# Set-up loads and steps in another order: a convolution, attention and mixture-of-experts kernel on one core

## The chip, the core and the metric

The kernel runs on one core of a Trainium2 chip. A core has a matrix engine (TensorE, PE in the profile), a vector engine (VectorE, DVE), an activation engine (ScalarE, ACT), a general engine (GpSimd, POOL) and a queue engine (SyncE, SP) that mainly issues DMAs. Each engine runs its own instructions in order, and waits on semaphores for what other engines and DMAs produce. ScalarE and GpSimd can issue DMAs too, from their own instruction streams.

The metric is the device time of one execution in microseconds (us). Before the change it is 3165.85 us, the median of three runs (3164.92 to 3170.51).

## What is computed

The input x is 8 images of 56 x 56 positions with 256 channels. Layer 0 sends it through 32 parallel paths, each a 1x1 convolution to 4 channels, a 3x3 convolution in these 4, and a 1x1 convolution back to 256, each followed by a batch norm and a ReLU, and adds up the paths and x. Layer 1 normalises, applies a linear attention over the positions of one image, normalises again and sends every position to the best 2 of 8 experts. Cut to what matters:

```
h = relu(bn1(x @ w1 + b1))                  # per path, 256 -> 4
h = relu(bn2(conv3x3(h, w2) + b2))          # per path, 4 -> 4
h = relu(bn3(h @ w3 + b3))                  # per path, 4 -> 256
x = relu(sum of h over the 32 paths + x)
t = x as tokens; n = layer_norm(t)
t = t + n + q @ (k^T v / N)                 # 8 heads, q = n, k and v normalised per head
t = t + moe(layer_norm(t))                  # router, best 2 of 8 experts, gelu
```

## The kernel before

**Tiling.** The 8 images are cut into 56 chunks of 8 rows, 448 positions each. Work runs in slots, one per chunk (the loop `for s in range(S + A + 1)` near the end of the function). Slot s computes the third convolution of chunk s (`pair`, L643 to L653, and `sum_paths`, L664), and beside it the first convolution of chunk s+2 (`conv1_steps`), the taps and the second convolution of chunk s+1 (`spread_taps`, `conv2_steps`), and, from the ninth slot on, attention and experts of earlier chunks. So before slot 0 can start, the set-up has to do the first convolution of chunks 0 and 1 and the second convolution of chunk 0, beside preparing all the weights.

**Order.** On TensorE, ScalarE and VectorE the instructions stand in the order in which the code issues them (`manual_schedule`). On SyncE and GpSimd a scheduler places them, by when it reckons that their inputs are there. Each of these two then also runs strictly in the order that came out.

**The set-up, in the code's order.**
- First weights W1 and the batch-norm rows are loaded, and `load(0)` (L87) loads the first chunk; `load` is called again in `conv1_steps` for the next chunk as soon as a chunk has been transposed. There is one input buffer (`xin`, one tile), so a load also waits for TensorE's transposes (L276) of the chunk before.
- GpSimd makes `ident` and the masks (`group_mask`, L138 to L143), the powers of the batch norms (L157), later the zero borders of h1 (L251 to L254), `path_mask` and `picks`.
- V3, G3, B3, M3, Be3 and W3 are loaded (L200, L215), VectorE works out scale and shift of the third batch norm, and the results are re-laid by eight small DMAs to `g3` and `bias3` (L206).
- The second weights come as twelve small DMAs to `W2s` (L233), 32 rows of 3 times 4 numbers each, 1.5 KB; VectorE spreads them into `W2t` (L241).
- `all_of(conv1_steps(0), conv1_steps(1))` (L353) runs the first convolutions (transposes L276, copies L279, products L287, activation L290 into `h1`), and `spread_taps(0)` copies shifted rows of h1 to the taps `R` with three DMAs (L310), two by SyncE and one by ScalarE.
- The third weights follow: `tp_mask` (L379), `spread`, `tp_g3` (L383), `W3s` (L384), products `tp_w3` (L390, L391), `W3hl` (L392).
- Then the biases of the third batch norm: `pmod`, `pdiv`, `b4` (L403 to L414) on VectorE, `tp_b3` (L419) on TensorE, `b3t` and `nb3` (L423, L424).
- Only then comes `all_of(conv2_steps(0))` (L425): twelve products (L323), the activation to `h2` (L332), its halves `hi` and `lo` (L340, L341), which four DMAs (L345) re-lay into `hl` for the third convolution: the two of lo by ScalarE, the two of hi by SyncE.
- `tp_sb` (L429) and `sumb`, and the output biases of the experts: `b2s` is loaded (L438), split into `b2hl` and `b2l`, and b2l stored into b2hl by a DMA (L441). With that the memory of the set-up is given back, and later tiles, `r` of L647 among them, are placed in it.
- Loads that attention needs: `kw_c`, `kb_c` (L461), `vw_b`, `vb_b` (L466), and the router weights `rwc` (L477), which are centred by four products with `mean_of` (L480) and two subtractions (L482).

Of the kernel before, what the change touches and what calls it, by code (L numbers as in the profile page):

```python
# [8 lines left out]
F32 = mybir.dt.float32  # L9
# [4 lines left out]
ALU = mybir.AluOpType  # L14
# [7 lines left out]
SYNC = mybir.DependencyInfo(mybir.DependencyClass.Sync, mybir.DependencyReason.DATA)  # L22
# [3 lines left out]
def kernel(  # L26
# [24 lines left out]
    nc = tc.nc  # L51
    B, N, C = x.shape
# [3 lines left out]
    E = w1.shape[0]  # L56
    HC = 32
    NH = C // HC
    P = 128
    NF = C // P  # L60
# [18 lines left out]
    ps_mm = ctx.enter_context(tc.tile_pool(name="ps_mm", bufs=7, space=PSUM))  # L79


    xs_in = {}

    def load(s):
        b, c = divmod(s, NCH)
        X = xin.tile([T, KT, C], F32, tag="xi", name=f"xi_{s}")
        nc.sync.dma_start(  # L87
            out=X, in_=x[b, c * CH : (c + 1) * CH, :].rearrange("(k q) c -> q k c", q=T)
        )
        xs_in[s] = X  # L90

    xtp = ctx.enter_context(tc.tile_pool(name="xtp", bufs=4))
# [15 lines left out]
    for g in range(NG):  # L108
        nc.scalar.dma_start(
            out=bn2s[32 * g : 32 * g + 32],  # L110
            in_=bn2[32 * g : 32 * g + 32].rearrange("(a e) k -> e a k", a=4),
# [118 lines left out]
    W2s = setup.tile([3 * 32, NG, 3, D], F32, name="W2s")  # L230
    for dx in range(3):
        for g in range(NG):
            nc.sync.dma_start(  # L233
                out=W2s[dx : 3 * 32 : 3, g],
                in_=W2[32 * g : 32 * g + 32].rearrange(
                    "q (dy dx o) -> dx q dy o", dy=3, dx=3
                )[dx],
            )
# [20 lines left out]
    def all_of(*parts_of_slot):  # L259
        for steps in parts_of_slot:  # L260
            for _, fn in steps:
                fn()
# [52 lines left out]
    def conv2_steps(s):  # L315
        ps = []

        def taps_of(dy):
            if dy == 0:
                ps.append(ps_mm.tile([P, 512], F32, tag="mm", name=f"c2_{s}"))  # L320
            R = tapped[s]
            for g in range(NG):
                nc.tensor.matmul(  # L323
                    ps[0][32 * g : 32 * g + 32, :CH],
                    W2t[:, g, dy, :],
                    R[:, g, :].rearrange("q (r w) -> q r w", w=W58)[:, dy : dy + ROWS, :HW],
                    start=(dy == 0), stop=(dy == 2),
                )
            if dy == 2:
                del tapped[s]  # L330
                h2 = split.tile([P, CH], F32, tag="h2", name=f"h2_{s}")
                nc.scalar.activation(h2, ps[0][:, :CH], AF.Relu, bias=sh2, scale=sc2)  # L332
                h2s[s] = h2

        def halves():

            h2 = h2s[s]
            hi = split.tile([P, CH], F32R, tag="hi", name=f"hi_{s}")
            lo = split.tile([P, CH], F32R, tag="lo", name=f"lo_{s}")
            nc.vector.tensor_copy(hi, h2)  # L340
            nc.vector.tensor_tensor(lo, h2, hi.bitcast(F32), ALU.subtract)  # L341
            hl = hlp.tile([P, NQ, CH], F32R, tag="hl", name=f"hl_{s}")
            for v, part in enumerate((hi, lo, hi, lo)):
                queue = nc.scalar if s == 0 and v % 2 else nc.sync
                queue.dma_start(out=hl[v : P : 4, :, :].bitcast(F32), in_=part.bitcast(F32))  # L345
            h2s[s] = hl

        return [
            (0.8, lambda: taps_of(0)), (0.8, lambda: taps_of(1)), (0.8, lambda: taps_of(2)),
            (0.8, halves),  # L350
        ]

# [25 lines left out]
    tp = ps_mm.tile([P, 512], F32, tag="mm", name="tp_mask")  # L378
# [3 lines left out]
    tp = ps_mm.tile([P, 512], F32, tag="mm", name="tp_g3")  # L382
# [5 lines left out]
    for ab in range(NQ):  # L388
        tp = ps_mm.tile([P, 512], F32, tag="mm", name=f"tp_w3_{ab}")
# [8 lines left out]
            ALU.mult,  # L398
        )


    pmod = setup.tile([NP, NPL], F32, name="pmod")
    nc.vector.tensor_reduce(  # L403
# [12 lines left out]
        )  # L416
    tp = ps_mm.tile([P, 512], F32, tag="mm", name="tp_b3")
    for cg in range(NCG):
        nc.tensor.matmul(  # L419
            tp[:, cg * 8 : cg * 8 + 8],  # L420
            b4[:, cg].rearrange("q p c -> q (p c)"), pdiv, start=True, stop=True,
        )
    nc.vector.tensor_copy(b3t, tp[:, : NCG * 8].rearrange("q (g n) -> q g n", n=8))  # L423
    nc.vector.tensor_scalar_mul(nb3, b3t, -1.0)  # L424
    all_of(conv2_steps(0))  # L425

    for f in range(NF):
        tp = ps_mm.tile([P, 512], F32, tag="mm", name=f"tp_sb_{f}")
# [26 lines left out]
    tables = ctx.enter_context(tc.tile_pool(name="tables", bufs=1))  # L455


    def column(src, name):

        t = const.tile([P, NF], F32, name=name)  # L460
        nc.sync.dma_start(out=t, in_=src.rearrange("o (f c) -> c (o f)", c=P))  # L461
        return t

    def bcast(src, name):
        t = const.tile([P, C], F32, name=name)
        nc.sync.dma_start(out=t, in_=src.to_broadcast([P, C]))  # L466
        return t

    kw_c, kb_c = column(kw, "kw_c"), column(kb, "kb_c")
# [3 lines left out]
    mean_of = const.tile([P, P], F32, name="mean_of")  # L473
    nc.gpsimd.memset(mean_of, 1.0 / C)

    rwc = const.tile([P, NF, E], F32, name="rwc")
    nc.sync.dma_start(out=rwc, in_=rwT.rearrange("(f c) e -> c f e", c=P))  # L477
    tp = ps_mm.tile([P, 512], F32, tag="mm", name="tp_rw")
    for f in range(NF):
        nc.tensor.matmul(tp[:, :E], mean_of, rwc[:, f, :], start=(f == 0), stop=(f == NF - 1))  # L480
    for f in range(NF):
        nc.vector.tensor_sub(rwc[:, f, :], rwc[:, f, :], tp[:, :E])  # L482

# [74 lines left out]
    for e in range(M):  # L560
# [6 lines left out]
        out=below, in_=below, compare_op=ALU.is_ge, fill=0.0, base=-1,  # L567
# [8 lines left out]
        out=earlier, in_=earlier, compare_op=ALU.is_ge, fill=0.0, base=-1,  # L576
# [919 lines left out]
    for s in range(S + A + 1):  # L1496
        a = s - A
        work_of = []
        era = " alone" if s < A else ""
        if s <= S:  # L1500
            work_of.append((0.0, 1.0 if is_chunk(s) else 0.1, conv3_steps(s)))
        if is_chunk(s + 2):
            work_of.extend(at("conv1" + era, conv1_steps(s + 2)))
        if is_chunk(s + 1):
            work_of.extend(at("taps" + era, [(0.0, lambda: spread_taps(s + 1))]))
            work_of.extend(at("conv2" + era, conv2_steps(s + 1)))
        if is_chunk(s - 1):
            if s < S:
                work_of.extend(at("end" + era, end_steps(s - 1)))
            else:  # L1510
                work_of.append((0.12, 0.99, end_steps(s - 1)))
        if is_chunk(a + 1):
            work_of.extend(at("fetch", [(0.0, lambda: fetch(a + 1))]))
        if is_chunk(a):
            opens = a % NCH == 0
            if opens:
                work_of.extend(at("image", image_steps(a // NCH)))
            if a + A > S:
                work_of.extend(at("attention first last" if opens else "attention last", attn_steps(a)))
            else:  # L1520
                work_of.extend(at("attention first" if opens else "attention", attn_steps(a)))
        work_of.extend(left)
        left = []
        if waiting and (len(waiting) == 2 or waiting[-1] % NCH == NCH - 1):
            last_image = waiting[-1] >= S - NCH
            compute, scatters = route_steps(waiting)
            rt = places["route" if s < S else "route last"]
            work_of.append((rt[0], rt[1], compute))
            if last_image:
                work_of.append((places["scatter last"][0], 0.995, sum(scatters, [])))  # L1530
            else:
                work_of.append((places["scatter"][0], 0.995, scatters[0]))
                left = [(0.0, places["scatter"][1], steps) for steps in scatters[1:]]
            if waiting[-1] in closing:
                work_of.append((places["plan"][0], places["plan"][1], plan_steps(closing.index(waiting[-1]))))
            waiting = []
        while r + 1 < len(closing) and known_in[r + 1] <= s:
            r += 1
        if r >= 0 and r + 1 < len(closing):
            goal = upto + (known_after[r] - 2 - upto) // (known_in[r + 1] - s)  # L1540
            if r + 2 < len(closing):
                goal = min(known_after[r] - 2, goal if s < known_in[1] else tiles_by(s))
            work_of.append((places["tiles"][s <= known_in[r]], places["tiles"][2], moe_steps(upto, goal)))
            upto = goal
        if 1 <= s <= E:
            work_of.append((0.5, 0.5, [(0.0, lambda: copy_weights(s - 1))]))
            work_of.append((0.8, 0.8, [(0.0, lambda: empty_rows(s - 1))]))
        if s == S + 1:
            apart.append(s)
        issue(*work_of)  # L1550
        if is_chunk(a):
            waiting.append(a)
# [60 lines left out]
```

## Time and profile before

| What | Value |
|---|---|
| median of three runs | 3165.85 us |
| the profiled execution | 3194.13 us |
| its span, first to last instruction | 3192.3 us |
| mean granted clock of TensorE, share of full | 0.962 |
| scatters on GpSimd, L1120 | 448, 957 ns each |
| adding scatters on GpSimd, L1413 | 420, 1573 ns each |

The span is what the profile's times are counted in; the profiled execution is somewhat longer than an execution without a profile. Stretches of the set-up, us busy of each engine, with the clock that TensorE was granted:

| Stretch, us | PE | DVE | ACT | POOL | PE clock |
|---|---|---|---|---|---|
| 0 to 13 | 4.96 | 5.83 | 3.07 | 9.83 | 1.00 |
| 13 to 26 | 5.22 | 3.46 | 2.04 | 2.58 | 0.61 |
| 26 to 40 | 10.14 | 7.61 | 0.00 | 0.00 | 0.70 |
| 40 to 53 | 7.07 | 2.68 | 1.87 | 0.00 | 0.50 |
| 53 to 83 | 28.66 | 20.03 | 18.25 | 0.00 | 0.90 |

In the first four stretches the load passes from engine to engine, and TensorE is busy 27.4 of 53 us. In the fifth, slot 0, TensorE is busy nearly throughout.

In the profile's lines a name such as `c`, `h` or `tx` is a program's tile name with its numbers left out, so c stands for the first, second and third convolution alike, and the line number tells them apart. SPq and ACTq mark the issuing of DMAs by SyncE and ScalarE. A 32-bit matrix product is recorded in two passes, so the twelve products L323 appear as `x24`.

### The profile page before, as it was taken

What the parts mean: (1) busy time and instruction counts of PE and PEld (TensorE: products, weight loads), DVE (VectorE), ACT (ScalarE), POOL (GpSimd) and SP (SyncE); (2) the same over time, 40 slices, a digit from 0 to 9 for tenths busy, and PEclk for the clock granted to TensorE, in tenths of its full rate; (3) what the DMA queues carried; (4) which work ended last, traced back from release to release, by engine and by line L of the source; (5) the groups of instructions that cost most, each with busy time, mean ns of one, the idle gap of its engine ahead of it and who ended that gap; (6) DMA issues with size and microseconds to landing.
All of it is one profiled execution on the core that took longest, in us unless ns stands there. A gap on an engine that the chain in (4) does not pass through costs nothing.

```text
span 3192.3 us, 53679 instructions
## 1 busy us (share of the span) xinstructions
PE 2924.8 (92%) x16677; PEld 1663.9 (52%) x16677; DVE 2173.6 (68%) x5743; ACT 1919.8 (60%) x3827; POOL 1844.5 (58%) x1363
## 2 busy tenths in 40 slices
PE   6999888888999999999999999999999997887798
PEld 3334334333455555455555555555555555776677
DVE  4787887787877687776877777777778784433200
ACT  2666665556666666566666766566656654454455
POOL 1233254455566675756756666666663556677677
PEclk7999998899999999999999999999999998998899
DMA  2543344344556666667665766667756666898897
GB/s 68 156 127 123 120 133 127 112 146 152 158 163 163 190 175 177 168 177 192 184 184 155 203 184 169 179 164 197 191 161 181 176 160 152 210 250 205 202 223 179
DMA packets 322669, 537.53 MB, mean 168 GB/s; under 512 B 41152, under 2 KB 232784, under 8 KB 322384
## 3 DMA queue, kind: packets, MB, share of 16 engines
q1 hardware_dynamic: 239808, 429.91, 44.4%
q0 software_dynamic: 81984, 103.45, 17.8%
q8 instruction: 133, 2.18, 0.3%
q14 instruction: 152, 1.25, 0.1%
q10 hardware_dynamic: 592, 0.76, 0.1%
HBM read 248.01 MB, written 192.55 MB: 138 GB/s over the span
## 4 chain that ended last, share of the span: by engine, by line
PE 68%; DVE 10%; issue 4%; ACT 3%; POOL 3%; DMA 2%; another core or an unknown queue 0%; ACTq 0%; SPq 0%; POOLq 0%; DVEq 0%
PE c L643 12%; PE ph L1375 11%; PE su L664 11%; PE py L1395 9%; PE at L939 7%; PE kv L813 3%; DVE r L651 3%; PE te L1335 3%; PE c L323 2%; PE py L1391 2%; POOL hsd L777 2%; PE c L287 2%; ACT r L648 2%; PE tu L712 1%; PE tx L276 1%
## 5 line engine op out<-in xcount | busy, mean ns | idle before, releaser
L651 DVE SCALAR_TENSOR_TENSOR r<-c,nb,r 128x448 f32<-128x448 f32 x1792 | 1131.2, 677 | 446.4 <-ACT r L648 414.4
L648 ACT ACTIVATE r<-c,b3t 128x448 f32<-128x448 f32 x1792 | 1038.5, 634 | 333.0 <-PE c L643 314.9
L1413 POOL DMA_INDIRECT out_dram<-y,index x420 | 660.5, 1573 | 342.7 <-ACT y L1399 221.5
L643 PE MATMUL c<-hl,W3hl 64*128 64x448 f32 x3584 | 690.4, 427 | 52.7 <-ACT r L648 19.3
L1120 POOL DMA_INDIRECT regions<-pay,rrowi x448 | 428.9, 957 | 311.9 <-PE c L643 198.5
L664 PE MATMUL su<-r,gather 128*32 128x448 f32 x3584 | 558.0, 566 | 42.8 <-DVE r L651 34.6
L643 PEld LDWEIGHTS c<-hl,W3hl 64*128 64x128 f32 x3584 | 328.2, 188 | 482.6 <-issue 242.0
L1375 PE MATMUL ph<-eT,w 128*128 128x256 f32 x1680 | 453.2, 401 | 38.1 <-issue 15.1
L1399 ACT ACTIVATE y<-py,rows 128x256 f32<-128x256 f32 x420 | 196.7, 474 | 438.9 <-PE py L1395 327.8
L1395 PE MATMUL py<-w,hT 128*128 128x256 f32 x1680 | 432.0, 381 | 7.0 <-issue 6.3
L1375 PEld LDWEIGHTS ph<-eT,w 128*128 128x128 f32 x1680 | 306.0, 196 | 169.0 <-issue 77.0
L1379 ACT ACTIVATE hT<-ph,w 128x256 f32<-128x256 f32 x420 | 197.9, 476 | 252.2 <-PE ph L1375 127.6
L777 POOL TENSOR_TENSOR hsd<-hsd,half 112x36 f32<-112x36 f32 x49 | 303.3, 6190 | 70.5 <-DVE hsd L775 69.6
L1395 PEld LDWEIGHTS py<-w,hT 128*128 128x128 f32 x1680 | 290.3, 191 | 36.6 <-issue 7.5
L939 PE MATMUL at<-tab,tT 128*112 128x272 f32 x896 | 266.2, 421 | 15.1 <-ACT r L648 6.1
L738 POOL TENSOR_TENSOR norm<-t,hmean 112x512 f32<-112x512 f32 x112 | 121.4, 1164 | 245.5 <-PE c L643 125.0
L664 PEld LDWEIGHTS su<-r,gather 128*32 128x32 f32 x3584 | 101.6, 109 | 250.2 <-DVE r L651 107.9
L939 PEld LDWEIGHTS at<-tab,tT 128*112 128x112 f32 x896 | 150.8, 182 | 94.1 <-issue 33.1
L943 DVE SCALAR_TENSOR_TENSOR X<-at,rs,X 112x256 f32<-112x256 f32 x224 | 107.0, 478 | 122.4 <-PE at L939 60.8
L1391 PE MATMUL py<-b2hl,own 128*128 128x256 f32 x420 | 179.1, 426 | 6.7 <-ACT y L1399 2.8
L1065 POOL TENSOR_TENSOR rq<-ebase,rq 112x8 f32<-112x8 f32 (+1 forms) x32 | 51.2, 1600 | 227.0 <-DVE rq L1064 227.0
L1339 ACT COPY eT<-te 128x512 f32<-128x512 f32 x210 | 123.5, 588 | 60.5 <-PE te L1335 40.6
(261 smaller groups left out, 3160.4 us busy)
## 6 DMA issues: line engine op xcount, KB each, us to landing
w<-Wd SPq DMA_DIRECT2D x210, 513.0 KB
rows<-regions SPq DMA_DIRECT2D x210, 259.0 KB
xi<-in_x_dram SPq DMA_DIRECT2D x56, 448.0 KB
hl<-hi SPq DMA_DIRECT2D x112, 224.0 KB
tTs<-u SPq DMA_DIRECT2D x56, 448.0 KB
ts<-t SPq DMA_DIRECT2D x56, 448.0 KB
tT<-tTs SPq DMA_DIRECT2D x56, 448.0 KB
X<-ts SPq DMA_DIRECT2D x56, 448.0 KB
```

Source lines behind the costliest of these rows:

```text
L643: product = nc.tensor.matmul(tiles[g][:, :CH], W3hl[rows, ab, cg, :], hl[rows, ab, :], start=True, stop=True)
L648: nc.scalar.activation(r, tiles[0][:, :CH], AF.Relu, bias=b3t[:, cg, 2 * ab : 2 * ab + 1])
L651: nc.vector.scalar_tensor_tensor(r, tiles[1][:, :CH], nb3[:, cg, 2 * ab + 1 : 2 * ab + 2], r, op0=ALU.max, op1=ALU.add,)
L664: nc.tensor.matmul(ps[32 * c4 : 32 * c4 + 32, :CH], gather, unit.pop((s, 4 * u + c4)), start=(ab == 0), stop=(ab == NQ - 1),)
L777: nc.gpsimd.tensor_tensor(sd, sd, half[:T, :].rearrange("q (k h) -> q k h", k=KT), ALU.pow)
L939: nc.tensor.matmul(ps, tT[:, f, k * T : (k + 1) * T], tables_of[b][:, f, :], start=(f == 0), stop=(f == NF - 1),)
L1120: ins = nc.gpsimd.indirect_dma_start(out=regions[n], out_offset=bass.IndirectOffsetOnAxis(ap=v["row_i"][:, (m - group[0]) * KT + k, n : n ...
L1375: nc.tensor.matmul(ps, w[:, f * C + hf * P : f * C + (hf + 1) * P], eT[:, f, :], start=(f == 0), stop=(f == NF - 1),)
L1379: nc.scalar.activation(hT[:, hf, :], ps, AF.Gelu, bias=w[:, 2 * NF * C + hf : 2 * NF * C + hf + 1])
L1391: nc.tensor.matmul(ps, own.to_broadcast([P, P]), b2hl, start=True, stop=False)
L1395: nc.tensor.matmul(ps, hT[:, f, h * P : (h + 1) * P], w[:, (NF + f) * C : (NF + f + 1) * C], start=False, stop=(f == NF - 1),)
L1413: ins = nc.gpsimd.indirect_dma_start(out=out_rows, out_offset=at, in_=y[:, h, :], in_offset=None, compute_op=ALU.add, **partial,).ins
```

## The change

The twelve loads of W2s are issued by GpSimd instead of SyncE. The second convolution of chunk 0 is put ahead of the biases of the third batch norm. The load of chunk 3 waits for the `lo` half of chunk 0 (`halved`), and the loads of kw_c, kb_c, vw_b, vb_b and rwc wait for the last product of tp_b3 (`last_made`). The router's centring becomes a function that is called at the start of slot 1. Nothing of what is computed changes.

```diff
@@ load(s)
-        nc.sync.dma_start(
+        ins = nc.sync.dma_start(
             out=X, in_=x[b, c * CH : (c + 1) * CH, :].rearrange("(k q) c -> q k c", q=T)
-        )
+        ).ins
+        if s == 3:
+            tc.add_manual_dep(ins, halved[0].name, SYNC, reason="not needed by the first chunk")
@@ second weights
     for dx in range(3):
         for g in range(NG):
-            nc.sync.dma_start(
+            nc.gpsimd.dma_start(
                 out=W2s[dx : 3 * 32 : 3, g],
@@ conv2_steps, halves
-            nc.vector.tensor_tensor(lo, h2, hi.bitcast(F32), ALU.subtract)
+            ins = nc.vector.tensor_tensor(lo, h2, hi.bitcast(F32), ALU.subtract).ins
+            if s == 0:
+                halved.append(ins)
@@ after W3hl, ahead of pmod
+    all_of(conv2_steps(0))
...
-        nc.tensor.matmul(
+        product = nc.tensor.matmul(
             tp[:, cg * 8 : cg * 8 + 8],
             b4[:, cg].rearrange("q p c -> q (p c)"), pdiv, start=True, stop=True,
         )
+    last_made = product.ins
...
     nc.vector.tensor_scalar_mul(nb3, b3t, -1.0)
-    all_of(conv2_steps(0))
@@ loads of attention and router
+    def not_yet(ins):
+
+        tc.add_manual_dep(ins, last_made.name, SYNC, reason="not needed by the first chunk")
...
-        nc.sync.dma_start(out=t, in_=src.rearrange("o (f c) -> c (o f)", c=P))
+        not_yet(
+            nc.sync.dma_start(out=t, in_=src.rearrange("o (f c) -> c (o f)", c=P)).ins
+        )
...
-        nc.sync.dma_start(out=t, in_=src.to_broadcast([P, C]))
+        not_yet(nc.sync.dma_start(out=t, in_=src.to_broadcast([P, C])).ins)
...
-    nc.sync.dma_start(out=rwc, in_=rwT.rearrange("(f c) e -> c f e", c=P))
-    tp = ps_mm.tile([P, 512], F32, tag="mm", name="tp_rw")
-    for f in range(NF):
-        nc.tensor.matmul(tp[:, :E], mean_of, rwc[:, f, :], start=(f == 0), stop=(f == NF - 1))
-    for f in range(NF):
-        nc.vector.tensor_sub(rwc[:, f, :], rwc[:, f, :], tp[:, :E])
+    not_yet(nc.sync.dma_start(out=rwc, in_=rwT.rearrange("(f c) e -> c f e", c=P)).ins)
+
+    def center_router():
+        tp = ps_mm.tile([P, 512], F32, tag="mm", name="tp_rw")
+        for f in range(NF):
+            nc.tensor.matmul(tp[:, :E], mean_of, rwc[:, f, :], start=(f == 0), stop=(f == NF - 1))
+        for f in range(NF):
+            nc.vector.tensor_sub(rwc[:, f, :], rwc[:, f, :], tp[:, :E])
@@ the loop over slots
+        if s == 1:
+            center_router()
```

More of the change, by code (lines that the diff above doesn't have):

```diff
@@ L82 @@
     xs_in = {}
+    halved = []
     def load(s):
```

## The prediction, made before the changed kernel had run

> **What bounds the kernel now.** I read the engine table of the page first. TensorE is busy 92% of the span, VectorE 68%, ScalarE 60%, so what counts in the long middle is the order of TensorE's work, and the change leaves that alone. The clock row comes next: one slice of forty, the first, stands out.
>
> ```profile
> PE 2924.8 (92%) x16677; PEld 1663.9 (52%) x16677; DVE 2173.6 (68%) x5743; ACT 1919.8 (60%) x3827; POOL 1844.5 (58%) x1363
> PEclk7999998899999999999999999999999998998899
> ```
>
> A slice is 80 us, and the set-up lies in the first. The chain of waits cannot be followed into it (its first piece is at 294 us), so the timeline of the first 60 us carries the case. Columns: start, length, engine, line, operation; in brackets the idle time before it.
>
> ```profile
> 7.66 7.71 SPq L233 DMA_DIRECT2D W2s<-in_W_dram  x12
> 15.48 0.52 SPq L87 DMA_DIRECT2D xi<-in_x_dram  x1
> 19.12 1.76 PE L276 MATMUL tx<-ident,xi 112*128 112x112 f32 x8 [7.91 <-DMA xi<-in_x_dram]
> 23.90 0.42 PE L379 MATMUL tp_mask<-ident,path_mask 128*32 128x128 f32 x1
> 26.71 0.42 DVE L384 TENSOR_TENSOR W3s<-W3s,tp_g 128x256 f32<-128x256 f32 x1 [8.68 <-PE tp_g L383]
> 35.90 3.55 PE L419 MATMUL tp_b<-pdiv,b 32*128 32x8 f32 x16 [2.92 <-DVE b L414]
> 39.38 4.71 PE L323 MATMUL c<-R,W2t 96*32 96x448 f32 x24
> 44.16 0.73 ACT L332 ACTIVATE h<-c,sh,sc 128x448 f32<-128x448 f32 x1 [18.24 <-PE c L323]
> 47.01 0.34 SPq L87 DMA_DIRECT2D xi<-in_x_dram  x1
> 47.45 1.34 SPq L345 DMA_DIRECT2D hl<-hi  x2
> 52.91 1.12 PE L643 MATMUL c<-hl,W3hl 64*128 64x448 f32 x4 [5.93 <-DMA hl<-hi]
> ```
>
> The reader sees three delays, one after another. Twelve W2s issues hold SP for 7.71 us, so the second chunk's input is issued at 15.48 and TensorE stands idle until 19.12. The first second convolution (L323) runs behind the bias products (L419) though its taps R were issued at 24.93. And the copies of its result (hl) leave SP behind a 448 KB input load, so the first third-convolution product waits 5.93 us. From 52.91 on, work is steady: TensorE busy 28.7 of the next 30 us.
>
> [...] a scatter (L1120) takes 0.95 us with 0.30 us to the next, an adding scatter (L1413) 1.57 and 0.30. No direct one is in this trace. [...] L323's 24 records take 4.71 us at 39.38 (granted clock 0.50) and 2.46 us at 71.62 (1.00).
>
> **The change, part by part.**
>
> *W2s leaves SP.* 7.71 us of issuing go from SP; input 1 is then released by TensorE's eight transposes of input 0 (done at 7.99) and issued at about 8.1. In the trace it takes 3.6 us from issue to transpose (15.48 to 19.12), so 11.7; L276 to the end of h1's second part takes 24.87 - 19.12 = 5.75, so 17.5 in place of 24.87.
>
> *W2s on GpSimd.* In the built order the twelve stand between bn1's power (L157) and the four borders of h1 (L251 to L254); behind these come path_mask and picks. The first taps (R) wait for the borders, tp_mask for path_mask, so all of them now wait for the twelve issues. Price: [...] a plain DMA of 96 short pieces is nearest to the 112-row scatter, 0.95 + 0.30 = 1.25, less its index; I take 1.1. Twelve make 13.2 us. From the end of bn1's power at 5.24: 13.2 + the four small ones left between them (0.30 + 0.25 + 0.57 + 0.25) = 19.9. Then borders 0.5, path_mask 0.23, picks 0.94, first select 0.53, own 0.2, second select 0.53: path_mask is ready at 22.8, where TensorE used to take it at 23.90. So GpSimd takes SP's place as the limit, about one microsecond earlier.
>
> *From the mask to W3.* tp_mask to W3s is 26.71 - 23.90 = 2.81 now; ScalarE's copy between them starts 1.35 us after tp_mask's end, because a taps issue (0.68) and h1 stand before it. Both are now over by 21.2, which gives 1.25 back: 22.9 + 2.81 - 1.25 = 24.45. VectorE arrives in time: W2t ends near 22.4, picks (0.90) 23.3, own4 24.0, all by the rows of before. W3s is 2.3 us early; so is the end of tp_w3 (6.27 us later): 30.7. Taps issued at 20.4 to 21.7 take at most 6 us (24.93 to about 31 with other loads): 27, in time.
>
> *Second convolution ahead of biases.* From tp_w3's end at 30.7, TensorE's clock is already up (the products at 31.95 to 32.98 take 0.6 where the first take 1.06), so I take 2.46 for L323, 4.71 if not: 33.2. h2 34.05, hi 34.5, lo 35.1. VectorE then makes pmod, pdiv and b4: 1.33 (34.43 to 35.76), 36.5. tp_b3 0.1 + 3.5: 40.1. The transposes of bias3 and chunk 2 take 46.97 - 44.02 - 0.87 (tp_rw, moved out) = 2.1: 42.3. The first L643 starts at 42.3 in place of 52.91, 10.6 early; 8.4 with the slow clock.
>
> *Loads held back.* hl is issued from 34.5 with no input load ahead. Before, 1344 KB (hl and an input) took 46.01 to 52.9; 896 KB at that rate plus the start take about 6 us: 40.6, hidden by tp_b3 with 1.7 us over. The column and broadcast loads wait for tp_b3 (40.1), and b2hl's store follows them on SP: four issues take 2.45 (27.25 to 29.70), it is issued at 42.6, and lands near 45. The first ScalarE r (L648) writes where b2l lay and so waits for it; it would want to start at 43.2. What is queued behind it is r 1 and then h1 of chunk 2, which must wait anyway for L287's 3.35 us (to 46.8). Two r (1.16) from 45 end at 46.2, so it is hidden by 0.6; up to 1.1 us is lost if L287 runs at full rate, which itself saves 1.6. Input 3 is issued near 44 and used 30 us later: nothing.
>
> *Router centring in slot 1.* Four products and two subtractions, 1.02 us at half clock, 0.5 at full: at most 0.5 back.
>
> Sum: 10.6, less 0.5 for slot 1, less 0.3 as a small share of the 2.2 us that a slow clock in L323 would cost: 9.8 us. On the profile's own time: span 3192.3 to 3182.5 (with what lies around it, 3194.13 to 3184.3). The runs' median lies 0.9% below the profiled execution; the set-up is a fixed stretch at the start, so I subtract the same from it: 3165.85 - 9.8 = 3156.0. All later waits are relative (product to activation, slot to slot), so a shift of the start goes to the end whole.
>
> **Rivals.**
>
> Dearer GpSimd issues. Each 0.1 us adds 1.2 to path_mask. At 1.5 to 1.87 the mask comes 4.8 to 9.2 later than reckoned and the gain is 5 to 0.6: about 3162.5. For it: the adding scatter's 1.87. Against: it has 128 rows and an addition.
>
> Cheaper issues. At 0.7 the mask is there at 18.0 and SP's own row (g3, bias, input 2, then R at 19.3) and R's landing near 26 become the limit as well (tp_w3 would end at 25.9): a gain near 14.6, 3151.
>
> [...]
>
> The start is shifted but the time is not: 3165.85. For it: the chain of waits shows nothing before 294 us. Against: TensorE's 28.7 busy of 30 us right after the set-up.
>
> **How the numbers follow.** Forecast (gain 6.5 to 13) 0.60; cheaper 0.12; dearer 0.17; no shift 0.05[...]. A measurement of this kernel can tell about 0.2%, 6.3 us, from no change. Faster by more: 0.60 + 0.12 = 0.72; within it 0.17 + 0.05 = 0.22; slower 0.06. The range takes the cheap case's 14.6 and a little run-to-run spread on one side, and all but the end of the dear one (1.4) on the other: 3150.5 to 3164.5.
>
> **What would show it.** Right: input 1's transposes near 12 us; POOL rows for W2s with a pitch near 1.1; tp_mask near 23; L323 near 31 in 2.5 us, tp_b near 36.5; first L643 near 42; first r near 45. Wrong: a pitch over 1.5, an idle ScalarE before h1 of chunk 2 because b2hl is late, or slot 0 starting early while slot 8 does not.

## The result, and the profile after

| | Before | After |
|---|---|---|
| median of all runs, 7 each | 3167.61 us (3164.92 to 3172.83) | 3150.42 us (3146.32 to 3159.09) |
| profiled execution | 3194.13 us | 3157.97 us |
| its span | 3192.3 us | 3156.2 us |
| mean granted clock | 0.962 | 0.966 |

After over before is 0.9949, with a 95% interval of 0.9935 to 0.9964: about 16.2 us of 3167.6 less, between 11 and 21. The two medians are 17.2 us apart. The forecast was a gain of 9.8. The median, 3150.42, lies 0.1 us under the low end of the stated range (3150.5). So not the case held most likely came (a gain of 6.5 to 13), but the rival with cheaper issues, held at 0.12, which had put the time at 3151.

The same timeline as before, now of the changed kernel (columns: start, length, engine, line, operation; in brackets the idle time before it). Its lines are 3 to 16 higher: L323 became L326, L419 L425, L643 L657, L648 L662.

```profile
7.97 5.43 POOL L236 DMA_DIRECT2D W2s<-in_W_dram  x10
7.95 0.33 SPq L88 DMA_DIRECT2D xi<-in_x_dram  x1
11.86 0.99 PE L279 MATMUL tx<-ident,xi 112*128 112x112 f32 x8 [0.71 <-DMA xi<-in_x_dram]
13.09 1.77 PE L290 MATMUL c<-xT,W1s 128*128 128x448 f32 x4 [0.24 <-ACT xT L282]
16.15 0.30 PE L384 MATMUL tp_mask<-ident,path_mask 128*32 128x128 f32 x1 [1.29 <-POOL path_mask L146]
17.53 0.42 DVE L389 TENSOR_TENSOR W3s<-W3s,tp_g 128x256 f32<-128x256 f32 x1 [0.37 <-PE tp_g L388]
17.98 1.46 DVE L391 CAST W3h<-W3s 128x256 fp32r<-128x256 f32 x1
25.95 2.46 PE L326 MATMUL c<-R,W2t 96*32 96x448 f32 x24
29.66 1.20 SPq L350 DMA_DIRECT2D hl<-hi  x2
31.59 3.27 PE L425 MATMUL tp_b<-pdiv,b 32*128 32x8 f32 x16 [3.18 <-DVE b L420]
36.73 1.11 PE L657 MATMUL c<-hl,W3hl 64*128 64x448 f32 x4
40.23 1.16 ACT L662 ACTIVATE r<-c,b3t 128x448 f32<-128x448 f32 x2 [2.86 <-DMA vb_b<-in_vb_dram]
```

All three delays of before are gone. Input 1 is issued at 7.95 instead of 15.48; the second convolution runs right behind the third weights, in 2.46 us at a granted clock of 1.00; and the first third-convolution product (L657) waits for no copy and starts at 36.73 instead of 52.91, 16.2 us early. GpSimd's twelve issues take 6.9 us in all, not 13.2, so the mask is taken at 16.15 where 22.9 was reckoned.

The steps beside the forecast, in us from the span's start:

| Step | Before | Forecast | After |
|---|---|---|---|
| transposes of input 1 | 19.12 | 11.7 | 11.86 |
| tp_mask | 23.90 | 22.9 | 16.15 |
| W3s | 26.71 | 24.45 | 17.53 |
| second convolution | 39.38 | 30.7 | 25.95 |
| tp_b3 | 35.90 | 36.5 | 31.59 |
| first L643 / L657 | 52.91 | 42.3 | 36.73 |
| first r (L648 / L662) | 53.78 | 45 | 40.23 |

**A mark to judge single executions by.** The runs of one kernel lie up to 14 us apart (3145.36 to 3159.09 for the changed one), in the last experiments up to 24 (3145.69 to 3169.47 for one edited kernel), so the time of one execution can't price a part of the set-up. What can is the ReLU over chunk 0's sum, the first instruction in which all of slot 0 has come together. In the kernel before:

```profile
88.93 0.95 ACT L700 ACTIVATE u<-u 128x896 f32<-128x896 f32 x1
```

and in the changed one:

```profile
72.97 0.95 ACT L714 ACTIVATE u<-u 128x896 f32<-128x896 f32 x1
```

So 88.93 and 72.97: 16.0 us. The same mark of chunks 1 to 6 comes 15.9 to 16.0 us early too, up to 293 us. From chunk 8 on the distance between the two profiles wanders (13.3 at chunk 12, 9.6 at chunk 18, 24.0 at chunk 55); the last experiment deals with that.

### The profile page after: what moved, and what is told of

The parts are those of the page before. It is cut to its first block, busy times and chain, and to the rows that moved or that the text cites. A ratio compares the mean times of both kernels' runs of the same rounds, so it can differ in the third digit from the quotient of the medians.

```text
span 3156.2 us, 53697 instructions
## 1 busy us (share of the span) xinstructions
PE 2916.8 (92%) x16677; PEld 1663.6 (53%) x16677; DVE 2177.3 (69%) x5743; ACT 1914.6 (61%) x3827; POOL 1854.2 (59%) x1375
## 3 DMA queue, kind: packets, MB, share of 16 engines
q14 instruction: 153, 1.25, 0.1%
## 4 chain that ended last, share of the span: by engine, by line
PE 62%; DVE 10%; POOL 7%; issue 4%; ACT 4%; DMA 4%; POOLq 0%; DVEq 0%; ACTq 0%; SPq 0%
PE c L657 12%; PE su L678 11%; PE ph L1389 9%; PE py L1409 8%; PE at L953 7%; POOL hsd L791 4%; DVE r L665 3%; PE kv L827 3%; DMA out_dram<-y,index 3%; PE te L1349 2%; PE py L1405 2%; PE c L326 2%; ACT r L662 2%; PE c L290 2%; POOL out_dram L1427 2%
## 5 line engine op out<-in xcount | busy, mean ns | idle before, releaser
L662 ACT ACTIVATE r<-c,b3t 128x448 f32<-128x448 f32 x1792 | 1039.3, 635 | 337.4 <-PE c L657 333.7
L657 PE MATMUL c<-hl,W3hl 64*128 64x448 f32 x3584 | 692.8, 429 | 42.6 <-ACT r L662 19.4
L657 PEld LDWEIGHTS c<-hl,W3hl 64*128 64x128 f32 x3584 | 328.2, 189 | 473.8 <-issue 225.9
L1405 PE MATMUL py<-b2hl,own 128*128 128x256 f32 x420 | 179.7, 428 | 22.9 <-ACT y L1413 16.3
L1405 PEld LDWEIGHTS py<-b2hl,own 128*128 128x128 f32 x420 | 79.9, 190 | 157.0 <-issue 45.3
L1349 PE MATMUL te<-ident,rows 128*128 128x128 f32 x840 | 137.5, 288 | 17.1 <-ACT y L1413 16.4
```

The lines of the kernel that those rows point to most:

```text
L657: product = nc.tensor.matmul(tiles[g][:, :CH], W3hl[rows, ab, cg, :], hl[rows, ab, :], start=True, stop=True)
L662: nc.scalar.activation(r, tiles[0][:, :CH], AF.Relu, bias=b3t[:, cg, 2 * ab : 2 * ab + 1])
L1349: nc.tensor.transpose(tp[:, f, h * P : (h + 1) * P], z[:, h, f * P : (f + 1) * P], ident)
L1405: nc.tensor.matmul(ps, own.to_broadcast([P, P]), b2hl, start=True, stop=False)
```

## The experiments

Theory A is the forecast's chain with the prices that the changed kernel's trace shows: GpSimd's path to the mask, the second convolution, the landing of hl and b2l's store stand in series, and each part of the change takes one of them away. The rivals carry other letters. "The mark" is the one above: 88.9 before, 73.0 after; it alone prices a part here, except where times are given too. In a second execution it came at 88.1 and at 72.3 (last experiment), so a difference under 0.8 us prices nothing.

The times of the single executions tell even less. On one chip the kernel before took 3197.0 us, and the changed kernel 3191.3 with W2s back, 3196.0 with the second convolution back, 3196.4 without holds and 3195.2 with twelve more issues: 0.6 to 5.7 us less, where the marks are 8.5 to 10.6 earlier. On another chip the kernel before took 3170.7, with W2s alone on GpSimd 3164.7, and the changed kernel 3151.1 with b2l's store first, 3147.5 with b4 ahead and 3168.4 with the late fills; the last two have the same mark. The unedited changed kernel was not run beside them.

### One part undone

**W2s back on SyncE.**

```diff
-            nc.gpsimd.dma_start(
+            nc.sync.dma_start(
                 out=W2s[dx : 3 * 32 : 3, g],
```

> The changed kernel with one part undone: the twelve W2s loads are issued by SyncE again. The mark is the start of the ReLU over chunk 0's sum (88.9 us before, 73.0 us changed). Theory A (each part of the change shortens a link of its own in one chain, and the W2s move is the largest): input 1 is issued at 15.5 us again, its transposes start at 19.1, tp_mask at 23.9, W3s at 26.7 in place of 17.5, and the first third-convolution product comes near 44.5 in place of 36.7: mark 80 to 82. Rival B (the second convolution's place and the free queue for hl do it all, W2s only moves idle time): mark 73 to 74.

The mark came at 80.2, 7.2 us later than in the changed kernel. Its timeline:

```profile
7.32 7.70 SPq L236 DMA_DIRECT2D W2s<-in_W_dram  x12
15.13 0.53 SPq L88 DMA_DIRECT2D xi<-in_x_dram  x1
18.68 1.75 PE L279 MATMUL tx<-ident,xi 112*128 112x112 f32 x8 [7.64 <-DMA xi<-in_x_dram]
```

The old first delay is back in full, and everything behind it moves with it (tp_mask 23.04, L657 43.86). The forecast's first step holds.

**Second convolution back behind the biases.**

```diff
-    all_of(conv2_steps(0))
     pmod = setup.tile([NP, NPL], F32, name="pmod")
...
     nc.vector.tensor_scalar_mul(nb3, b3t, -1.0)
+    all_of(conv2_steps(0))
```

> The changed kernel with one part undone: the second convolution of chunk 0 stands behind the bias products again. Theory A: tp_b3 runs at 29 to 32 us, the second convolution after it, at half clock (4.7 us) or not (2.5 us), hl is issued from 36 to 38 and the first third-convolution product waits for it until 42 to 44 in place of 36.7; part of it is given back because b2l's store is then no longer late: mark 77 to 81. Rival B: the same direction, but with the whole of the gain gone, mark near 88. Rival C (the W2s move alone carries the gain): mark 73 to 74.

The mark came at 80.4, 7.4 us later. The lines that carry it:

```profile
31.99 4.21 PE L326 MATMUL c<-R,W2t 96*32 96x448 f32 x24
37.45 1.20 SPq L350 DMA_DIRECT2D hl<-hi  x2
38.77 0.54 SPq L88 DMA_DIRECT2D xi<-in_x_dram  x1
44.21 1.12 PE L656 MATMUL c<-hl,W3hl 64*128 64x448 f32 x4 [6.86 <-DMA hl<-lo]
```

Two things return. The convolution starts behind the bias products, and takes 4.21 us in place of 2.46; and with nothing left to do behind it, TensorE waits 6.86 us for hl. So the biases' products are worth more as cover for the copies than they cost. Not all of the wait is hl's own: input 3, held for `lo` alone, goes out at 38.77 beside the copies. Here L656 starts 6.8 us after hl's first issue; in the two kernels below in which L657 waits for hl with input 3 issued later, it starts 4.3 to 4.5 us after.

**The loads not held back** (neither input 3 nor the columns, broadcasts and rwc).

```diff
-        if s == 3:
-            tc.add_manual_dep(ins, halved[0].name, SYNC, reason="not needed by the first chunk")
...
     def not_yet(ins):
-        tc.add_manual_dep(ins, last_made.name, SYNC, reason="not needed by the first chunk")
+        return ins
```

> The changed kernel without the holds: the load of chunk 3 and the loads of kw_c, kb_c, vw_b, vb_b and rwc wait for nothing but their buffers. In the order that is built, the five small loads then stand ahead of input 1 on SyncE (five issues, 2.5 to 4 us), and input 3 behind hl. Theory A: input 1's transposes come 3 to 5 us later than 11.9, but that link has slack, since GpSimd's path_mask is the later one until 16.1 us, so W3s is 2 to 4 us late; b2l's store is early, so the first r follows its product at once (1.2 us back): mark 73.5 to 76. Rival D (the holds are worth nothing): mark 71.8 to 73, by b2l's earlier store alone.

The mark came at 78.4, 5.4 us later, more than expected. SyncE's row and what waited for it:

```profile
8.03 0.43 SPq L470 DMA_DIRECT2D kw_c<-in_kw_dram  x1
...
10.55 0.40 SPq L88 DMA_DIRECT2D xi<-in_x_dram  x1
15.37 1.75 PE L277 MATMUL tx<-ident,xi 112*128 112x112 f32 x8 [4.41 <-DMA xi<-in_x_dram]
40.51 0.34 SPq L88 DMA_DIRECT2D xi<-in_x_dram  x1
40.94 0.80 SPq L445 DMA_DIRECT2D b2hl<-b2l  x1
44.60 1.16 ACT L660 ACTIVATE r<-c,b3t 128x448 f32<-128x448 f32 x2 [3.55 <-DMA b2hl<-b2l]
```

Once the twelve W2s issues have left SyncE, its scheduler puts the five small loads into the freed place, ahead of input 1. Input 1 is issued 2.6 us later than in the changed kernel and takes 4.8 us from issue to use instead of 3.9 (that the small loads' bytes do this was not shown), so the transposes come 3.5 us later, and the first third-convolution product 3.7 (40.41). At the other end, input 3 goes out ahead of b2l's store, and r starts 3.7 us after the store's issue instead of 2.5. The two kinds of holds were not taken off one by one. The forecast had credited only the hold on input 3, and looked at the others for what they delay; here these keep the place free.

### One part alone

**The kernel before with nothing but W2s on GpSimd.**

```diff
-            nc.sync.dma_start(
+            nc.gpsimd.dma_start(
                 out=W2s[dx : 3 * 32 : 3, g],
```

> The kernel before with one part of the change alone: the twelve W2s loads are issued by GpSimd. The mark is the start of the ReLU over chunk 0's sum (88.9 us before, 73.0 us changed). Theory A (the parts are links of one chain): in the built order the five small loads of attention and router take the freed place ahead of input 1, so W3s comes near 22.9 us as in the run without the holds, 3.8 earlier than before, and everything behind it keeps the old order: mark 84.5 to 86. Rival C (the W2s move alone carries the gain): mark 73 to 75. Rival B (it carries nothing): mark 88 to 89.

The mark came at 82.3: 6.6 us better than before, so more than A reckoned, and far from what B and C say. The five small loads stand ahead of input 1 here too (kw_c at 7.23, input 1 at 9.74), and at the end the old wait for hl is still there:

```profile
18.43 0.42 PE L379 MATMUL tp_mask<-ident,path_mask 128*32 128x128 f32 x1
31.34 1.98 PE L419 MATMUL tp_b<-pdiv,b 32*128 32x8 f32 x16 [3.19 <-DVE b L414]
33.25 4.71 PE L323 MATMUL c<-R,W2t 96*32 96x448 f32 x24
46.73 1.11 PE L643 MATMUL c<-hl,W3hl 64*128 64x448 f32 x4 [5.88 <-DMA hl<-hi]
```

So W2s's queue brings 6.6 alone, and 9.3 are left for the rest. Undone one by one the parts cost 7.2, 7.4 and 5.4, 20.0 together, where all of them brought 16.0: they lean on one another, and no part has a price of its own. The router's centring was not undone by itself.

### The price of a GpSimd issue

**Twelve more loads of the same shape on GpSimd, into a tile that nothing reads.**

```diff
+    W2x = setup.tile([3 * 32, NG, 3, D], F32, name="W2x")
+    for dx in range(3):
+        for g in range(NG):
+            nc.gpsimd.dma_start(
+                out=W2x[dx : 3 * 32 : 3, g],
...
```

> The changed kernel with twelve more loads of W2 on GpSimd right after the twelve, into a tile that nothing reads. Theory A (GpSimd's issues are the limit of the first 16 us, at 0.54 us each): 12 x 0.54 = 6.5 us more ahead of the borders of h1 and path_mask; tp_mask at 22.7 in place of 16.15, the taps' issue waits for the borders at 20.2, and the mark moves by 6 to 6.6 us, to 79 to 79.6. Rival E (SyncE's row of g3, bias3 and input 2, with the taps' issue at 18.0, is the limit, GpSimd has slack): the mark moves by less than 3 us.

The mark came at 79.1, 6.1 us later.

```profile
13.21 6.47 POOL L245 DMA_DIRECT2D W2x<-in_W_dram  x12
22.28 0.40 PE L393 MATMUL tp_mask<-ident,path_mask 128*32 128x128 f32 x1 [8.11 <-POOL path_mask L146]
```

6.47 us for twelve is 0.54 each, and tp_mask moved from 16.15 to 22.28, by 6.13. Here GpSimd alone is the limit: TensorE waits 8.11 us for the mask, and the delay reaches the mark undiminished. With twelve dearer by 0.54 each this is also very nearly the forecast's own world (twelve at 1.1): it gives a gain of 9.8 at the mark, and 9.8 was forecast. W3s comes at 24.28 (24.45 forecast), the second convolution at 31.98 (30.7), the first third-convolution product at 42.91 (42.3). That the sum is hit to 0.1 is luck: the stretch behind W3s took 1.45 us longer than reckoned, the steps behind it 1.3 less.

### The wait of the first r

**The small loads and input 3 held until b2l's store has landed**, instead of the store behind them.

```diff
-    nc.sync.dma_start(out=b2hl[E : 2 * E].bitcast(F32), in_=b2l.bitcast(F32))
+    stored = nc.sync.dma_start(out=b2hl[E : 2 * E].bitcast(F32), in_=b2l.bitcast(F32)).ins
+    halved[0] = stored
...
-        tc.add_manual_dep(ins, last_made.name, SYNC, reason="not needed by the first chunk")
+        tc.add_manual_dep(ins, stored.name, SYNC, reason="not needed by the first chunk")
```

> The changed kernel with the five small loads and the load of chunk 3 held until b2l's store has landed, in place of the last bias product and of lo. In the changed kernel the first r starts at 40.23 us, 3.5 us after its product, and the profile names the landing of vb_b as what it waited for. Theory A (it is b2l's store, issued at 37.74 behind the small loads): the store is issued near 36.3, r starts near 38.6, h1 of chunk 2 follows its product at 40.1, and the mark is 71.5 to 72.2. Rival F (it really is vb_b, or another of the small loads): these now land after 40.5, r starts near 42, and the mark is 74 to 75.

The mark came at 72.4.

```profile
35.78 0.79 SPq L447 DMA_DIRECT2D b2hl<-b2l  x1
39.28 0.43 SPq L479 DMA_DIRECT2D vb_b<-in_vb_dram  x1
37.83 1.16 ACT L663 ACTIVATE r<-c,b3t 128x448 f32<-128x448 f32 x2 [0.90 <-DMA b2hl<-b2l]
37.34 3.35 PE L290 MATMUL c<-xT,W1s 128*128 128x448 f32 x4
```

The changed kernel's profile puts the wait of the first r down to vb_b, the transfer that came last. Here r starts at 37.83, before vb_b is even issued, and 2.05 us after the store. So the releaser was b2l's store, which frees the memory that r takes, and the name in brackets was the wrong one of two. At the mark this brings nothing that can be told: 0.6 of the 2.4 that r came earlier, and outside theory A's 71.5 to 72.2. L290 took 3.35 us this time, as long as L287 at 20.75 in the kernel before, where the granted clock was 0.50 (in the changed kernel 2.26 us, at 0.77), and the activation of chunk 2 waits for that product. The fair comparison is the changed kernel's second profile, where L290 was as slow:

```profile
36.15 1.11 PE L657 MATMUL c<-hl,W3hl 64*128 64x448 f32 x4
37.19 3.35 PE L290 MATMUL c<-xT,W1s 128*128 128x448 f32 x4
38.79 1.16 ACT L662 ACTIVATE r<-c,b3t 128x448 f32<-128x448 f32 x2 [2.00 <-DMA vb_b<-in_vb_dram]
```

There the mark came at 72.3 though r waited 2.6 us; from the first third-convolution product to the mark it is 36.1 us in both.

### Two more waits taken out, and all of them together

**pmod, pdiv and b4 ahead of the second convolution.** In the changed kernel they stand behind it on VectorE, and TensorE idles 3.18 us for them (the tp_b line above).

```diff
-    all_of(conv2_steps(0))
     pmod = setup.tile([NP, NPL], F32, name="pmod")
...
             b4[:, :, pl, :], bias3.rearrange("q (g c) -> q g c", c=32), pmod[:, pl : pl + 1]
         )
+    all_of(conv2_steps(0))
```

> The changed kernel with VectorE's pmod, pdiv and b4 put ahead of the second convolution, where VectorE waits for h2 from 27.5 to 29.2 us; tp_b3 stays behind it. Theory A (TensorE's wait of 3.2 us for b4 is on the chain): tp_b3 starts near 28.5 to 28.9 in place of 31.6, the transposes of chunk 2 end near 34, and the first third-convolution product starts when hl has landed, near 35, in place of 36.7: mark 71 to 72. Rival G (hl's landing is already the limit, near 36.5): mark 72.5 to 73.

```profile
28.08 1.95 PE L425 MATMUL tp_b<-pdiv,b 32*128 32x8 f32 x16 [0.43 <-DVE b L418]
33.44 1.12 PE L657 MATMUL c<-hl,W3hl 64*128 64x448 f32 x4 [1.93 <-DMA hl<-lo]
```

The mark came at 71.9. The pause is 0.43 us, and the bias products take 1.95 us instead of 3.27. (With W2s alone they took 1.98 behind a pause of 3.19, and the second convolution behind them 4.71.) L657 starts 3.3 us earlier, now behind hl's landing; of this only 1.1 arrived, because the first r started at 38.09, 5.6 us after b2l's store had been issued behind the small loads (at 32.46; by the trace's semaphore records its last part landed at 37.91).

**GpSimd's fills held until the last bias product** (offs, code, below, ones, earlier and five pads; in the changed kernel they start at 17.7 us, and the first of them run beside the cast to W3h).

```diff
-        nc.gpsimd.memset(offs[:, e : e + 1], float(0 if e == 2 * E else e % E * CAPR + TR))
-        nc.gpsimd.memset(code[:, e : e + 1], float(E - e % E))
+        not_yet(nc.gpsimd.memset(offs[:, e : e + 1], float(0 if e == 2 * E else e % E * CAPR + TR)).ins)
+        not_yet(nc.gpsimd.memset(code[:, e : e + 1], float(E - e % E)).ins)
...
```

> The changed kernel with GpSimd's fills of offs, code, below, ones, earlier and the five pads held until the last bias product. Theory H (VectorE's conversion W3h at 17.98 us takes 1.46 us in place of 0.29 because GpSimd fills tables at that time): W3h takes 0.3, tp_w3 starts 1.2 to 1.4 us earlier, mark 71.5 to 71.9. Rival I (the conversion is slow for another reason): W3h stays near 1.4 and the mark at 73.

```profile
18.00 0.29 DVE L391 CAST W3h<-W3s 128x256 fp32r<-128x256 f32 x1
34.18 1.42 DVE L431 TENSOR_SCALAR nb<-b3t 128x64 f32<-128x64 f32 x1
36.34 2.61 DVE L535 CAST pos<-pos_i 128x2 f32<-128x2 int32 x1
36.44 0.80 SPq L447 DMA_DIRECT2D b2hl<-b2l  x1
39.16 1.16 ACT L662 ACTIVATE r<-c,b3t 128x448 f32<-128x448 f32 x2 [2.76 <-DVE row_code L540]
```

The mark came at 71.9. The cast is back at 0.29 us (1.46 in the changed kernel), and tp_w3 starts 1.15 us earlier. But the fills now meet VectorE's small operations behind the biases: nb takes 1.42 us (0.20 before), a cast of 128x2 numbers 2.61 (0.15). The slowness went with the fills. The name in brackets is again the wrong one: by the trace's semaphore records the last part of b2l's store landed at 38.98, and r starts 0.18 us later, as it does in the changed kernel (40.05 and 40.23). From the first third-convolution product (35.76) to the mark it is 36.1 us, so nothing was lost there. Of the 1.1 us at the mark 0.4 is left against the changed kernel's second profile, less than two executions differ by. So it is shown that the fills slow the cast, not that they cost the mark anything.

**All together**, the fills held only until the subtraction behind the cast.

```diff
-    nc.vector.tensor_sub(W3s, W3s, W3h.bitcast(F32))
+    parted = nc.vector.tensor_sub(W3s, W3s, W3h.bitcast(F32)).ins
...
+    def past_cast(ins):
+        tc.add_manual_dep(ins, parted.name, SYNC, reason="not beside the cast")
...
-        nc.gpsimd.memset(offs[:, e : e + 1], float(0 if e == 2 * E else e % E * CAPR + TR))
+        past_cast(nc.gpsimd.memset(offs[:, e : e + 1], float(0 if e == 2 * E else e % E * CAPR + TR)).ins)
...
```

> The changed kernel with four remaining waits of the set-up taken out together: b4 ahead of the second convolution, the small loads and input 3 held until b2l's store has been issued, and GpSimd's fills of offs, code, below, ones, earlier and the first pads held until VectorE has done the subtraction behind the W3h cast (not until after the biases, where they slowed VectorE's small operations). If the three gains add (theory J): the bias copies' 1.0, the first expansion's 0.6 and the cast's 1.1 come to 2.7, of which some is lost to the hl tiles' landing, which limited the first expansion at 33.4 when b4 alone was moved. ReLU of chunk 0's sum at 70.0 to 71.2 (73.0 in the changed kernel); W3h cast 0.3; first L657-type expansion 32.3 to 32.8; first r within 1.5 of its product's end. Rival K (the store of b2l or the hl tiles is now the limit of all): mark 71.7 to 72.4, no better than either change alone, and r waits for b2l again. Time against the changed kernel on the same chip: ratio 0.999 (J), equal (K); both are near what the spread between executions hides.

```profile
24.98 2.46 PE L326 MATMUL c<-R,W2t 96*32 96x448 f32 x24 [1.38 <-DMA R<-h]
32.97 1.11 PE L662 MATMUL c<-hl,W3hl 64*128 64x448 f32 x4 [2.59 <-DMA hl<-lo]
34.01 3.35 PE L290 MATMUL c<-xT,W1s 128*128 128x448 f32 x4
```

The mark came at 69.1, 3.9 us before the changed kernel's and a little better than theory J; K falls. The first r starts at 34.05, within 1.1 us of its product's start. What limits now is transfers: the taps R (1.38 us) and hl (2.59). In the times the 3.9 us can't be seen: 0.9948 of the time before (0.9935 to 0.9961), beside 0.9952 (0.9936 to 0.9968) for the changed kernel, measured together.

### Does the gain reach the end?

The changed kernel and the kernel before, once more and not edited.

> The changed kernel, not edited, beside the kernel before. Theory A (what the set-up gains at the first sum, 16.0, is kept to the end of the program): time 16 less, ratio 0.9949, and in this second profile the mark is again 72.5 to 73.5 and the marks of chunks 0 to 6 stand 15.5 to 16.5 earlier than in the first profile of the kernel before. Rival W (the shift of the later chunks belongs to the change): the marks of chunks 12, 18 and 55 are again 13.3, 9.6 and 24.0 early within 1. Under A they are anywhere between 5 and 30 early, since two executions of one kernel differ there by as much.

> The kernel before, not edited. Theory A with drift between executions: the marks of chunks 0 to 6 are those of its first profile within 0.5, and from the attention of the first image on they differ from them by 3 to 20, growing and falling, though not one instruction differs. Rival W: the marks of all chunks are those of the first profile within 1.

The changed kernel took 3153.61 us (6 runs) beside 3169.7 for the kernel before (11 runs), ratio 0.9952. The mark of chosen chunks, each kernel's second profile beside its first:

```
chunk            0      6      8     12     18     26     40     55
before        88.9  292.6  371.6  542.4  807.3 1207.0 1908.2 2662.9
before, 2nd   88.1  291.8  368.3  543.1  811.7 1204.3 1902.1 2653.0
after         73.0  276.6  354.2  529.1  797.7 1190.5 1888.2 2638.9
after, 2nd    72.3  275.9  353.1  524.0  792.7 1185.4 1883.1 2633.9
```

Two executions of the kernel before agree within 0.8 us up to chunk 6. Then the second comes 3.3 us earlier, 0.7 and 4.4 later, and 2.7, 6.1 and 9.9 earlier, and their spans by 23 us (3192.3 and 3169.1), without one instruction changed. So rival W falls: the wandering distance is there without the change, though whether it comes with the execution or with the chip was not told apart (that of the first profiles is not on record); against the first profile of the kernel before, the second of the changed one is 18.4 early at chunk 12 and 29.0 at chunk 55, not 13.3 and 24.0 (and 16.6 early at chunk 0, a little outside what was expected). That the start's 16 us arrive at the end is shown by the medians alone, and there within 11 to 21.

Where two such executions part can be seen. The stretches of both near chunk 7, where attention begins; columns: stretch, its length, busy us of PE, PEld, DVE, ACT, POOL with counts, granted clock, DMA share, GB/s. First profile of the kernel before:

```profile
325.00:333.00 8.00, 7.57 (x28) 3.86 (x28) 7.13 (x22) 3.16 (x5) 0.00 (x0) 0.57 0.07 26
333.00:341.00 8.00, 7.52 (x45) 3.69 (x44) 4.28 (x10) 5.04 (x9) 0.00 (x0) 0.86 0.75 203
```

Second profile:

```profile
325.00:333.00 8.00, 8.00 (x43) 3.70 (x42) 6.65 (x20) 4.99 (x9) 0.00 (x0) 0.79 0.16 60
333.00:341.00 8.00, 7.08 (x42) 3.89 (x39) 5.92 (x13) 5.30 (x10) 2.04 (x2) 1.00 0.64 169
```

TensorE had paused (1.20 and 2.11 us in the first; of the 8 us from 317 it was busy for 5.12 in the first and 4.69 in the second), and its clock comes back earlier in the second execution (0.79 against 0.57): 43 records in 8 us instead of 28. By the trace's clock records it ran at half clock for 6.8 us from 325.2 in the first, and for 3.4 us from 325.9 in the second. Why it came back earlier was not shown, nor that all of the wandering comes from such stretches. Nor is a profiled execution longer as such: the first of the kernel before lay 0.9% over its runs' median, but the second (3170.98 us beside 3169.7) and that of the changed kernel (3157.97, within its runs) do not.

## Why the forecast was too small

The chain was right and one price was not. At the mark 6.2 us more were won than forecast; the price of the issues alone makes 6.3, and the other terms lost 2.2 and won 2.0.

**W2s leaves SP: right.** Transposes of input 1 at 11.86 (11.7 forecast). h1's second part ended at 15.63, not 17.5, since L290 ran in 1.77 us, at a granted clock of 1.00, instead of 3.35 at 0.50 (TensorE had waited 0.71 us ahead of the transposes, and 7.91 in the kernel before).

**W2s on GpSimd: the place was right, the price was not.** This is the term that failed: 1.1 us an issue, taken from the indirect scatter's 0.95 + 0.30. Measured, all twelve issues of the changed kernel (minimum, median and maximum in ns, first and last start):

```profile
L236 POOL DMA_DIRECT2D W2s<-in_W_dram x12: 545/547/807, 4.8 to 12.9; - x12
```

They add up to 6.9 us where 13.2 was reckoned, and these 6.3 us are nearly the whole difference at tp_mask (22.9 - 16.15 = 6.75); the rest is mostly that bn1's power ended at 4.80 in this execution and not at 5.24. (The forecast's own terms for the end of the issues add up to 19.8, not 19.9; it changes nothing.) As forecast, GpSimd is what TensorE waits for there (1.29 us for path_mask), and the 24 issues show that the term is linear (12 more moved tp_mask by 6.13 us). The nearest row was the wrong one: one of these plain DMAs took 0.547 us in the median, little more than half of the indirect one's 0.952. The 0.06 held for a slower kernel was the author's estimate: by the forecast's own terms the gain is gone at 1.1 + 9.8 / 12 = 1.9 us an issue, and the longest took 0.81. VectorE was working beside most of them, but in short operations (0.37 us at most until the last issue); issues beside long ones were not measured.

**From the mask to the second convolution: 2.15 us longer than reckoned.** From W3s to L326 it is 8.42 us and not 6.27, so of the 6.9 us won over the forecast at W3s 4.75 were left. The cast to W3h took 1.46 us instead of 0.29 and tp_w3 started about 1.15 late; the rest is that only its last two products found the clock up (0.75 and 0.59 us at a mean granted clock of 0.86; those before, at 0.50, took 1.06 and more). The cast's part came from being early: GpSimd's short fills, which before lay ahead of it, now ran beside it. With the fills held, the cast took 0.29, and in the kernel with all waits out the stretch to the end of tp_w3 was 6.3 us again (17.33 to 23.60). Chance has a part in it: in the changed kernel's second profile the cast took 1.64 us, and yet L326 started 7.66 us after W3s (25.06). The forecast moved VectorE's work without looking at what GpSimd would be doing then.

**Second convolution ahead: right.** 2.46 us, at a granted clock of 1.00; from its start to the first L657, 10.8 us (11.6 forecast).

**hl and the loads held back: right, and worth more than said.** hl's landing is hidden by tp_b3 as forecast. The holds on the small loads had been counted as harmless; without any hold 5.4 us are lost, 3.7 of them by the first third-convolution product, by way of input 1, where the forecast saw nothing to win.

**b2l's store: mechanism right, outcome at its bound.** It was to be hidden by 0.6, with up to 1.1 lost if L287 (now L290) ran at full rate. It ran in 2.26 us (mean granted clock 0.77), ended at 40.03, and its activation started at 41.28 behind two r that had waited for the store: 1.25 lost, about what the faster product gave (1.1). In the second profile it took 3.35 us, and the activation followed at 40.59, 0.05 us behind its end: nothing lost, as forecast for a product of 3.35 us.

**Router centring: right.** tp_rw takes 0.61 us ahead of the mark, and from the first L657 (16.2 early) to the mark (16.0) no more than 0.2 was given back in all, where 0.8 had been set aside.

**The shift goes to the end whole: supported, not sharply.** To chunk 6 it is exact (15.9 to 16.0; 15.8 to 15.9 between the second profiles); for the end only the medians speak, within 11 to 21.

## What to carry to other kernels

Price an instruction by a row of its own kind, not by the nearest in name: an indirect DMA's 0.95 us and its gap stood for a plain one's 0.55, and that price was the main error. When a stage moves, look at what the neighbouring engine does at the new time, and which loads a scheduler will slip into the place that came free; holding those back was worth nearly as much as the move (5.4 and 7.2 us). Waits in series at a start are best judged by one early mark in the trace, since some us at the start can't be told from one execution's total.

## What the runs showed of the hardware

- The plain DMAs of 96 short pieces were issued by GpSimd 0.54 us apart (the first took 0.81 us), by SyncE 0.64 apart (7.71 us for twelve). An indirect one held GpSimd for 0.96 us and an adding one for 1.57, with 0.30 to the next where one followed directly on another.
- Single VectorE instructions took five to seventeen times as long beside GpSimd's fills. The cast of 128x256 took 1.46 us in the changed kernel and 0.29 with the fills held; where the held fills then ran, the scaling of 128x64 took 1.42 us (0.20 in the changed kernel) and the cast of 128x2 took 2.61 (0.15). The subtraction of two tensors behind the first cast showed it less: 0.66 us in the changed kernel, 0.43 in the kernel before.
- The same twelve products of the second convolution took 2.46 us in the changed kernel, at a granted clock of 1.00, and 4.71 us in the kernel before, at 0.50, where TensorE had waited 2.92 us ahead of the bias products before them. Put back behind the biases in the changed kernel they took 4.21 us. With W2s alone it was not the instructions next to the wait that were slow: the bias products just behind a pause of 3.19 us took 1.98 us, the second convolution behind them 4.71.
